# A cross-attention kernel: the queries' seven block products in transposed form, with the steady round in another order

## The chip, the cores and the metric

The kernel runs on one core of one Trainium2 chip. The metric is the device time of one launch in microseconds, as the median of several executions. The engines are TensorE (PE; its weight loads are shown as PEld), VectorE (DVE), ScalarE (ACT), GpSimd (POOL) and SyncE (SP, which here only issues DMAs). They run on their own instruction queues, each in program order, and wait for one another by semaphores.

## The reference

For each of 64 batches, with x of 256x512 and a context c of 256x384, all in float32:

```python
text_p  = x @ W_text + b_text            # queries, 256x512
audio_p = c @ W_audio + b_audio          # keys and values, 256x512
Q = layer_norm(text_p, g1, beta1)
K = layer_norm(audio_p, g2, beta2)
alpha = softmax(Q @ K.T / sqrt(512))     # 256x256
h = (alpha @ audio_p) @ W_out + b_out
out = layer_norm(h + x, g_out, beta_out)
```

## The kernel before, in words

Everything is float32 and all big products are made from fewer block products than the plain form has. The queries of a batch are a 2x2 block product (rows in two halves of 128, the inner 512 in two halves, the columns in two halves of 256) and take seven products instead of eight, each of two matmuls of 128x256. The keys (class `Thirds`) and the output projection, which is folded with the value projection (`y`, also `Thirds`), take fifteen products with columns in thirds of 171. The scores and the context's first part take seven products of 128 columns too.

The queries are class `Fork`. `SumX` makes the sums and differences of x's blocks on GpSimd (four instructions for each batch, into tile `xsum`), `weight_sums` those of the weights once (`wtsum`). Two PSUM banks, `fork[0]` and `fork[1]`, hold the four result blocks: `R`, `q1` in the first and `q2`, `q3` in the second. `Fork.seed` copies half of the bias into `R`; product one adds to `R`; `after_one` (ScalarE) copies `R` to `q1`; seven goes into `q3` and `after_seven` (ScalarE) takes it out into `s7`; six adds to `R`; `start_q3` (VectorE) writes `q3 = R + s7` and `step_r` (VectorE) moves `R` from one half of the bias to the other by `bt_step`; five adds to `R`; `after_five` (VectorE) writes `q2 = R + s7`; three, two and four finish `R`, `q1` and `q3`. `square` and `normalise` (ScalarE) then read the banks for the layer norm. `Thirds` works in the same way in four further banks (M, L, TU, N), which keys and output projection use in turn: for instance `take_m` and `start_u` (VectorE) read the two halves of bank M between `four` and `five`, and the third and fourth product of `five` write to these halves again.

The order of all work is written out by hand (a manual schedule): a prologue for the first batches, a steady round `for b in range(3, B - 3)`, 58 times, and an end. The steady round works on six batches at once: `q2`/`k2` are the queries and keys of batch b+2, `q3` is the first query product of batch b+3, `cT`/`xT`, `cs` and `x_new` are the transposed inputs and sums of batch b+3, `at` is the attention of batch b, `last` the context of b-1, `old` and `y` the output projection of b-2, `settled` the final layer norm of b-3 (`deviation`, `last_deviation`, `shift`, `settle`). A statement's place in that list sets its place in each engine's queue. The tiles of pool `work` have two buffers, those of `once` one.

The other names in the prediction: `after_six` is what follows six; `key_step`, `query_step`, `c_step`, `e_step`, `cs.add` and `x_new.add` are GpSimd sums, `z_step` are sums on VectorE or GpSimd; `turn` and `turn_e` are VectorE transposes of tiles that were stored to memory and fetched again (`store`, `fetch`, `store_e`, `fetch_e`: SP's queue); `copy_u` and `copy_n` (ScalarE) take U and N out of PSUM; `maxima` is a VectorE reduction over the scores; `affine_keys` and `affine_queries` are ScalarE. The rows of L541 are the small VectorE sums of helper `dve`, those of L1348 and L1357 are `shift` and `settle`.

Of the kernel before, what the change touches and what calls it, by code (L numbers as in the profile page):

```python
# [22 lines left out]
def kernel(  # L23
# [257 lines left out]
    def weight_sums(w_sb, n, name):  # L281

        w = [[w_sb[:, j * n : (j + 1) * n, k * H2 : (k + 1) * H2] for k in (1, 0)] for j in (0, 1)]
# [6 lines left out]
        ws = {1: w[0][0], 2: w[1][0], 3: w[1][1], 4: t[:, 3], 5: t[:, 0], 6: t[:, 1], 7: t[:, 2]}  # L290
        return {p: [ap[:, k, :] for k in range(n)] for p, ap in ws.items()}

    class SumX:

        def __init__(self, xT, engine=nc.gpsimd):
            n = DC // 2
            part = lambda i, j: xT[:, j * n : (j + 1) * n, bass.ts(i, P)]
            s = work.tile([P, 4, n, P], F32, tag="xsum", name="xsum")
            self.engine = engine
            self.steps = [  # L300
                (s[:, 2], part(0, 0), part(1, 0), ALU.subtract),
                (s[:, 0], part(1, 0), part(1, 1), ALU.add),
                (s[:, 1], s[:, 0], part(0, 0), ALU.subtract),
                (s[:, 3], part(0, 1), s[:, 1], ALU.subtract),
            ]
            ss = {
                1: part(0, 0), 2: part(0, 1), 4: part(1, 1),
                5: s[:, 0], 6: s[:, 1], 7: s[:, 2], 3: s[:, 3],
            }
            self.of = {p: [ap[:, k, :] for k in range(n)] for p, ap in ss.items()}  # L310

        def add(self, n=4):
# [404 lines left out]
    class Fork(Projection):  # L717

        R, q1 = fork[0][:, :H2], fork[0][:, H2:]
        q2, q3 = fork[1][:, :H2], fork[1][:, H2:]  # L720
# [7 lines left out]
        def seed():  # L728
            nc.scalar.copy(Fork.R, bt_sb[:, H2:])

        def product(self, n, place):
            for c, (side, w) in enumerate(zip(self.sides[n], self.weights[n])):
# [4 lines left out]
                    start=(n == 7 and c == 0),  # L737
# [7 lines left out]
        def seven(self):  # L745
            self.product(7, self.q3)
# [4 lines left out]
        def after_seven(self):  # L751
            self.s7 = once.tile([P, H2], F32, tag="s7", name="s7")
            nc.scalar.copy(self.s7, self.q3)
# [17 lines left out]
        def after_five(self):  # L771
            dve(self.q2, self.R, self.s7, ALU.add)
# [7 lines left out]
        def four(self):  # L780
            self.product(4, self.q3)

        def rest(self):
            self.three()
            self.two()
            self.four()
# [657 lines left out]
    bt_step = const.tile([P, H2], F32, tag='bt_step', name='bt_step')  # L1444
# [31 lines left out]
    xs_1.add(1)  # L1476
# [25 lines left out]
    nc.vector.tensor_tensor(bt_step, bt_sb[:, :H2], bt_sb[:, H2:], ALU.subtract)  # L1502
# [15 lines left out]
    q[1].start_q3()  # L1518
    fold_multiply(0, 3, 4)
    q[1].step_r()  # L1520
# [12 lines left out]
    xs[2].add(1)  # L1533
# [21 lines left out]
    q[1].three()  # L1555
    k2_0.start_t()
    cs[3].add(1)
    q[1].four()
# [37 lines left out]
    q2_0.start_q3()  # L1596
# [3 lines left out]
    xs[3].add(1)  # L1600
# [10 lines left out]
    q2_0.step_r()  # L1611
# [14 lines left out]
    q2_0.three()  # L1626
# [7 lines left out]
    q2_0.four()  # L1634
# [23 lines left out]
    q2_0.normalise([0])  # L1658
# [5 lines left out]
    xs[4].add(1)  # L1664
# [4 lines left out]
    q2_0.normalise([1])  # L1669
# [16 lines left out]
    q2_1.start_q3()  # L1686
    xs[4].add(1)
    k2_1.four()
    q2_1.step_r()
# [17 lines left out]
    q2_1.three()  # L1707
# [7 lines left out]
    q2_1.four()  # L1715
# [84 lines left out]
    q2_2.start_q3()  # L1800
    q2_2.step_r()
# [23 lines left out]
    q2_2.three()  # L1825
# [13 lines left out]
    q2_2.four()  # L1839
# [8 lines left out]
    xs[5].add(1)  # L1848
# [11 lines left out]
    q2_2.normalise([0])  # L1860
# [23 lines left out]
    q2_2.normalise([1])  # L1884
# [41 lines left out]
    for b in range(3, B - 3):  # L1926
        settled, old, last = att.pop(b - 3), att[b - 2], att[b - 1]
        old.context_two(0)
        old.context_two(1)
        q2 = q[b + 2]  # L1930
        old.z_part(2)
        old.copy_two()
        old.z_part(4)
        old.product_sums()
        at = att[b]
        x_old = x_rows[b - 2]
        old.z_part(3)
        old.add_c21()
        cT[b + 3] = turn_c(b + 3)
        old.copy_top()  # L1940
        q2.seven()
        old.z_step(0)
        last.context_sums()
        k2 = k[b + 2] = Thirds("k", b + 2, cs.pop(b + 2), wa_blocks, ba_sb, ba_delta)
        y = old.o
        at.affine_queries(1)
        k2.one()
        at.query_sums()
        k2.copy_n1()
        at.affine_queries(0)  # L1950
        at.query_step(0)
        old.z_step(7)
        old.z_step(1)
        old.z_step(2)
        q2.six()
        q2.after_seven()
        k2.start_t()
        at.open_scores()
        last.c_step(0)
        at.affine_queries(3)  # L1960
        k2.two()
        last.fetch_e()
        q2.start_q3()
        settled.totals()
        k2.three()
        old.z_step(3)
        k2.copy_t()
        q2.step_r()
        old.z_step(4)
        k2.start_l0()  # L1970
        at.score_part(1, 7)
        settled.deviation(1)
        k2.start_l1()
        xT[b + 3] = turn_x(b + 3)
        q2.five()
        at.affine_queries(2)
        k2.four()
        q2.after_five()
        cs[b + 3] = Sides(cT.pop(b + 3), "csum").add(0)
        x_new = SumX(xT.pop(b + 3))  # L1980
        k2.take_m()
        settled.deviation(0)
        k2.start_u()
        settled.shift(1)
        settled.last_deviation()
        cs[b + 3].add(1)
        old.z_step(5)
        var = small.tile([P, 4], F32, tag="var4", name="var")
        k2.five()
        k2.copy_n()  # L1990
        at.copy_p1()
        k[b + 1].turn([0])
        k2.leave_ends()
        q2.four()
        at.copy_p7()
        k2.copy_u()
        at.query_step(1)
        at.query_step(2)
        k2.middle_v()
        q2.square(var[:, :2], [1])  # L2000
        at.score_part(6)
        k2.leave_middle()
        q2.two()
        k2.middle_less()
        k2.leave()
        if b + 4 < B: load_c(b + 4)
        y.seed()
        at.query_step(3)
        at.add_p7(0)
        k[b + 1].turn([1])  # L2010
        if b + 4 < B: load_x(b + 4)
        k2.square(var[:, 2:], [0])
        if done: done.store()
        y.one()
        last.turn_e()
        q2.three()
        last.c_step(1)
        y.copy_n1()
        q3 = q[b + 3] = Fork(b + 3, x_new.of, wt_blocks)
        x_new.add(1)  # L2020
        cs[b + 3].add(1)
        last.open_context()
        last.weight_sums()
        at.score_part(5)
        old.z_step(6)
        k2.square(var[:, 2:], [1])
        last.e_step(0)
        q2.square(var[:, :2], [0])
        y.start_t()
        settled.settle(1)  # L2030
        at.add_p7(1)
        q[b + 1].turn()
        last.c_step(2)
        y.three()
        last.z_part(7)
        y.two()
        y.copy_t()
        att[b + 1] = Attention(b + 1)
        at.score_part(4)
        done = settled  # L2040
        scales_of(q2, k2, var)
        at.score_part(3)
        cs[b + 3].add(1)
        last.keep_z7()
        last.e_step(1)
        y.start_l1()
        last.z_part(1)
        last.e_step(2)
        q2.normalise([1])
        cs[b + 3].add(1)  # L2050
        at.score_part(2)
        att[b + 1].key_sums()
        last.c_step(3)
        y.start_l0()
        q2.normalise([0])
        last.copy_z1()
        settled.shift(0)
        x_new.add(1)
        at.maxima()
        cs[b + 3].add(1)  # L2060
        k2.normalise([0])
        y.four()
        y.take_m()
        k2.normalise([1])
        y.start_u()
        x_new.add(1)
        last.z_part(6)
        at.exponentials([0])
        at.exponentials([1])
        Fork.seed()  # L2070
        att[b + 1].affine_keys(2)
        cs[b + 3].add(1)
        att[b + 1].affine_keys(1)
        last.add_u3()
        y.five()
        cs[b + 3].add(1)
        settled.settle(0)
        att[b + 1].affine_keys(0)
        att[b + 1].affine_keys(3)
        y.plus_ends(x_old)  # L2080
        x_new.add(1)
        load_x_rows(b - 1)
        y.plus_middle(x_old, 1)
        y.last_11()
        q2.store()
        k2.seed()
        att[b + 1].key_step(0)
        k2.store()
        at.reciprocals()
        q3.one()  # L2090
        load_c_rows(b)
        y.plus_n0()
        last.z_part(5)
        q2.fetch()
        at.divide_e([1])
        at.divide_e([0])
        last.add_c22()
        y.last_01(x_old)
        at.store_e()
        q3.after_one()  # L2100
        att[b + 1].key_step(1)
        y.last_10()
        att[b + 1].key_step(2)
        k2.fetch()
        y.plus_middle(x_old, 0)
        y.last_00()
# [40 lines left out]
    q2_m3.start_q3()  # L2147
    k2_m3.four()
    at_m3.keep_p7()
    q2_m3.step_r()  # L2150
# [325 lines left out]
```

## Time and profile before

| what | value |
|---|---|
| three runs | 1336.13, 1336.77, 1336.94 us; median 1336.77 |
| profiled execution, span from first to last instruction | 1333.9 us |
| median less span | 2.87 us |
| mean granted TensorE clock | 1.000 |
| one steady round | 20.30 us |

The profiled execution is another one than the three that were timed; its own time is its span and the little that lies around it. "Busy" is the time in which an engine has an instruction in work. A row of the timeline has the start, the length, the engine, the line, the operation, what it writes and reads, and a count; a bracket says how long the engine had been idle before, and who released it. A float32 matmul appears as two records, so the two matmuls of one query product are "x4". A row of a group has total busy time and the mean length in ns behind the bar.

### The profile page before, as it was taken

What the parts mean: (1) busy time and instruction counts of PE and PEld (TensorE: products, weight loads), DVE (VectorE), ACT (ScalarE), POOL (GpSimd) and SP (SyncE); (2) the same over time, 40 slices, a digit from 0 to 9 for tenths busy, and PEclk for the clock granted to TensorE, in tenths of its full rate; (3) what the DMA queues carried; (4) which work ended last, traced back from release to release, by engine and by line L of the source; (5) the groups of instructions that cost most, each with busy time, mean ns of one, the idle gap of its engine ahead of it and who ended that gap; (6) DMA issues with size and microseconds to landing.
All of it is one profiled execution on the core that took longest, in us unless ns stands there. A gap on an engine that the chain in (4) does not pass through costs nothing.

```text
span 1333.9 us, 29733 instructions
## 1 busy us (share of the span) xinstructions
PE 1327.5 (100%) x8497; PEld 1246.6 (93%) x8497; DVE 1257.0 (94%) x3314; ACT 1174.8 (88%) x3310; POOL 1172.8 (88%) x1854
## 2 busy tenths in 40 slices
PE   9999999999999999999999999999999999999998
PEld 5899999999999999999999999999999999999996
DVE  6769999999999999999999999999999999999977
ACT  4899898898898998998988988989988989889886
POOL 5789999999998998998999999989989989999964
PEclk9999999999999999999999999999999999999999
DMA  9988898898988988988888988988889888889783
GB/s 214 250 235 239 230 268 238 241 261 237 250 251 225 261 248 241 259 248 244 249 241 239 264 236 246 260 241 246 252 225 268 246 236 258 242 241 257 213 248 116
DMA packets 448970, 322.23 MB, mean 242 GB/s; under 512 B 153765, under 2 KB 381349, under 8 KB 448806
## 3 DMA queue, kind: packets, MB, share of 16 engines
q1 hardware_dynamic: 448710, 320.20, 85.7%
q8 instruction: 68, 1.11, 0.4%
q14 instruction: 96, 0.79, 0.2%
q10 hardware_dynamic: 96, 0.13, 0.0%
HBM read 203.57 MB, written 116.65 MB: 240 GB/s over the span
## 4 chain that ended last, share of the span: by engine, by line
PE 98%; DMA 1%; DVE 0%; SPq 0%; issue 0%; POOL 0%; ACT 0%; DVEq 0%
PE ps_f L733 29%; PE ps_m L557 16%; PE ps_sc L884 14%; PE ps_n L557 11%; PE ps_u L557 8%; PE ps_z L1033 7%; PE ps_l L557 5%; PE ps_z L1095 5%; PE ps_sc L823 1%; DMA ba<-in_L_xattn_b_audio_dram 0%; DMA c<-in_ctx_dram 0%; PE ps_l L244 0%; PE ps_f L440 0%; PE ps_fold L244 0%; PE ps_m L244 0%; PE ps_sc L900 0%
## 5 line engine op out<-in xcount | busy, mean ns | idle before, releaser
L352 POOL TENSOR_TENSOR csum<-csum,cT 128x256 f32<-128x256 f32 x310 | 202.0, 652 | 0.6
L733 PE MATMUL ps_f<-wtsum,xsum 128*128 128x256 f32 x756 | 194.0, 379 | 0.0
L527 ACT ACTIVATE qT<-qT,columns 128x256 f32<-128x256 f32 x256 | 152.9, 599 | 0.0
L733 PEld LDWEIGHTS ps_f<-wtsum,xsum 128*128 128x128 f32 x756 | 131.8, 191 | 11.4 <-issue 0.7
L869 POOL TENSOR_TENSOR qsum<-qT 128x256 f32<-128x256 f32 x118 | 86.4, 732 | 58.3 <-ACT qT L527 56.7
L1158 ACT ACTIVATE junk<-yr,nm 128x512 f32<-128x512 f32 x124 | 88.6, 715 | 55.0 <-POOL nm L1140 54.8
L527 ACT ACTIVATE kT<-kT,columns 128x256 f32<-128x256 f32 x256 | 133.7, 595 | 0.4 <-DVE kT L76 0.4
L884 PE MATMUL ps_sc<-kT,qT 128*128 128x128 f32 x928 | 131.8, 275 | 0.0
L733 PE MATMUL ps_f<-wt,xT 128*128 128x256 f32 x504 | 129.5, 379 | 0.0
L1357 DVE SCALAR_TENSOR_TENSOR yr<-yr,rstd,beo 128x512 f32<-128x512 f32 x120 | 123.0, 1025 | 0.1
L884 PEld LDWEIGHTS ps_sc<-kT,qT 128*128 128x128 f32 x928 | 121.3, 192 | 0.0
L1348 DVE SCALAR_TENSOR_TENSOR yr<-yr,nm,go 128x512 f32<-128x512 f32 x124 | 109.7, 885 | 0.0
L794 ACT ACTIVATE junk<-ps_f 128x512 f32<-128x512 f32 x126 | 75.2, 597 | 35.7 <-PE ps_f L733 32.2
L884 PEld LDWEIGHTS ps_sc<-ksum,qsum 128*128 128x128 f32 x696 | 100.6, 191 | 6.0
L884 PE MATMUL ps_sc<-ksum,qsum 128*128 128x128 f32 x696 | 105.8, 275 | 0.0
L733 PEld LDWEIGHTS ps_f<-wt,xT 128*128 128x128 f32 x504 | 88.4, 190 | 6.7
L314 POOL TENSOR_TENSOR xsum<-xT 128x256 f32<-128x256 f32 x124 | 91.0, 735 | 1.9 <-DVE xT L76 1.9
L541 DVE TENSOR_TENSOR ps_l<-ps_m,t 128x171 f32<-128x171 f32 x248 | 82.8, 334 | 8.7 <-ACT t L605 3.0
L520 DVE STREAM_TRANSPOSE kT<-kq 128x512 f32<-128x512 f32 x122 | 85.4, 702 | 2.0 <-DMA kq<-kd 2.0
L488 ACT ACTIVATE kr<-kr,rstd 128x512 f32<-128x512 f32 x126 | 84.7, 727 | 0.0
L460 ACT ACTIVATE junk<-kr 128x512 f32<-128x512 f32 x126 | 80.9, 642 | 0.3
L804 ACT ACTIVATE qr<-ps_f,rstd 128x512 f32<-128x512 f32 x126 | 80.2, 690 | 0.2
(302 smaller groups left out, 4670.1 us busy)
## 6 DMA issues: line engine op xcount, KB each, us to landing
kd<-kr SPq DMA_DIRECT2D x64, 512.0 KB, 3.4
kq<-kd SPq DMA_DIRECT2D x256, 128.0 KB, 3.8
qd<-qr SPq DMA_DIRECT2D x64, 512.0 KB, 3.2
qq<-qd SPq DMA_DIRECT2D x256, 128.0 KB, 4.3
xq<-in_x_dram SPq DMA_DIRECT2D x252, 128.0 KB, 2.8
x<-in_x_dram SPq DMA_DIRECT2D x63, 512.0 KB, 5.0
out_dram<-yr SPq DMA_DIRECT2D x62, 512.0 KB, 3.8
cq<-in_ctx_dram SPq DMA_DIRECT2D x252, 96.0 KB, 2.4
```

The costliest lines, as they stand in the source:

```text
L314: self.engine.tensor_tensor(*step)
L352: nc.gpsimd.tensor_tensor(*step)
L520: nc.vector.transpose(self.T.rearrange("p k (q t j) -> p t q k j", t=self.nt, j=SQ)[:, t], self.sq[:, t * NQ : (t + 1) * NQ].rearrange("p ...
L527: nc.scalar.activation(self.T[:, k, :], self.T[:, k, :], AF.Identity, bias=bet[:, k : k + 1], scale=gam[:, k : k + 1],)
L557: nc.tensor.matmul(place, lhsT=self.sides.of[n], rhs=self.weights[n], start=(n == 14), stop=True, skip_group_check=True,)
L733: nc.tensor.matmul(place, lhsT=side, rhs=w, start=(n == 7 and c == 0), stop=True, skip_group_check=True,)
L869: nc.gpsimd.tensor_tensor(*self.steps[n])
L884: nc.tensor.matmul(self.place(t, m), lhsT=self.qsides[n][:, c], rhs=self.ksides[n][:, c], start=False, stop=True, skip_group_check=True,)
L1033: nc.tensor.matmul(self.zp[{1: 0, 2: 0, 4: 2}.get(n, 1)], lhsT=self.asides[n], rhs=self.bsides[n], start=(n == 7), stop=True, skip_group_c ...
L1158: nc.scalar.activation(junk, self.y[:, t, :], AF.Square, bias=self.nm[:, t : t + 1], accum_out=self.ssq[:, t : t + 1],)
L1348: nc.vector.scalar_tensor_tensor(row, row, self.nm[:, t : t + 1], go_sb, ALU.add, ALU.mult)
L1357: nc.vector.scalar_tensor_tensor(self.y[:, t, :], self.y[:, t, :], self.r[t], beo_sb, ALU.mult, ALU.add)
```

## The change

The block products of the queries are rearranged: the blocks of x and of the weights take each other's roles in the seven-product scheme. x's sums become three instructions, the first of them 512 columns wide; the weights' sums stay four. The roles of the PSUM blocks change: `R` and `q4` lie in `fork[1]`, `q1` and `q2` in `fork[0]`. `Fork.seed` is one copy of 512 columns: the first half of the bias goes to `R`, and the difference of the halves, which VectorE makes once in the prologue in place of `bt_step`, to `q4`. Product seven adds to that seed, so that `s7` carries the step between the halves; `step_r` is gone. `after_six` writes `q2`, `after_five` writes `q4`, and four adds to `q2`. Where the prologue and the end named the old steps they name the new ones, and three and four change places there.

```diff
-        add(t[:, 0], w[0][1], w[0][0], ALU.subtract)
-        add(t[:, 1], w[1][1], t[:, 0], ALU.subtract)
-        add(t[:, 2], w[1][1], w[0][1], ALU.subtract)
+        add(t[:, 0], w[0][1], w[1][1], ALU.add)
+        add(t[:, 1], t[:, 0], w[0][0], ALU.subtract)
+        add(t[:, 2], w[0][0], w[0][1], ALU.subtract)
         add(t[:, 3], w[1][0], t[:, 1], ALU.subtract)
...
-                (s[:, 2], part(0, 0), part(1, 0), ALU.subtract),
-                (s[:, 0], part(1, 0), part(1, 1), ALU.add),
-                (s[:, 1], s[:, 0], part(0, 0), ALU.subtract),
-                (s[:, 3], part(0, 1), s[:, 1], ALU.subtract),
+                (
+                    s[:, 0:2],
+                    xT[:, :, P:].rearrange("p (j c) l -> p j c l", j=2),
+                    xT[:, :n, :].rearrange("p c (m l) -> p m c l", m=2),
+                    ALU.subtract,
+                ),
+                (s[:, 2], part(1, 1), s[:, 0], ALU.subtract),
+                (s[:, 3], part(0, 1), s[:, 2], ALU.subtract),
...
-        R, q1 = fork[0][:, :H2], fork[0][:, H2:]
-        q2, q3 = fork[1][:, :H2], fork[1][:, H2:]
+        R, q4 = fork[1][:, :H2], fork[1][:, H2:]
+        q1, q2 = fork[0][:, :H2], fork[0][:, H2:]
...
-            nc.scalar.copy(Fork.R, bt_sb[:, H2:])
+            nc.scalar.copy(fork[1], bt_sb)
...
-                    start=(n == 7 and c == 0),
+                    start=False,
...
-        def start_q3(self):
-            dve(self.q3, self.R, self.s7, ALU.add)
-
-        def step_r(self):
-            dve(self.R, self.R, bt_step, ALU.add)
-
         def after_six(self):
-            self.start_q3()
-            self.step_r()
+            dve(self.q2, self.R, self.s7, ALU.add)
...
+    nc.vector.tensor_tensor(bt_sb[:, H2:], bt_sb[:, H2:], bt_sb[:, :H2], ALU.subtract)
...
-    nc.vector.tensor_tensor(bt_step, bt_sb[:, :H2], bt_sb[:, H2:], ALU.subtract)
```

The steady round's list is written in another order throughout. The new list, cut to the statements that the prediction speaks of:

```python
old.z_part(2); old.z_part(4); old.context_two(0); ...
q2.seven(); q2.after_seven(); k2.one(); ...
old.z_part(3); old.context_two(1); old.copy_two(); old.z_step(0); ...
q2.six(); q2.after_six(); k2.three(); ...; k2.two(); load_c(b + 4); ...
q2.five(); ...; xT[b + 3] = turn_x(b + 3); k2.four(); ...; last.fetch_e()
at.query_step(0); at.query_step(1); ...; q2.after_five(); at.score_part(1, 7); ...
k2.five(); ...; q2.three(); settled.shift(1); q2.two(); ...
k2.copy_n(); at.copy_p7(); ...; settled.last_deviation(); k2.copy_u()
k2.leave_ends(); k2.leave_middle(); k2.middle_v(); old.z_step(4); k2.middle_less()
k[b + 1].turn([1]); ...; last.turn_e(); at.score_part(6); y.one(); ...; q2.four()
cs[b + 3].add(1); ...; last.e_step(0); ...; at.add_p7(0); old.z_step(6); last.e_step(1)
y.start_t(); settled.shift(0); at.score_part(5); ...; at.add_p7(1); y.three(); last.z_part(7); ...
settled.settle(1); y.two(); at.score_part(4); load_c_rows(b); x_new.add(1); ...
y.start_l0(); ...; at.score_part(2); at.score_part(3); ...; last.z_part(1); ...
y.start_l1(); att[b + 1].q.turn(); y.four(); ...; settled.settle(0); y.take_m(); ...
y.start_u(); ...; at.maxima(); ...; last.z_part(6); ...; Fork.seed(); ...
y.five(); load_x(b + 4); ...; last.z_part(5); ...; x_new.add(1); q3.one(); ...
x_new.add(1); ...; q3.after_one(); k2.seed(); ...; att[b + 1].affine_keys(0); ...
att[b + 1].key_step(0); ...; at.store_e(); k2.fetch(); att[b + 1].key_step(2)
```

More of the change, by code (lines that the diff above doesn't have):

```diff
@@ L780, in four @@
         def four(self):
[L781 to L786, printed above, removed]
+            self.product(4, self.q2)
         def square(self, var=None, tiles=range(2)):
@@ L1633 @@
     k[1].fetch()
-    q2_0.four()
+    q2_0.three()
     at_0.score(1, 2)
@@ L1706 @@
     q2_1.two()
-    q2_1.three()
+    q2_1.four()
     at_1.affine_keys(0)
@@ L1824 @@
     q2_2.two()
-    q2_2.three()
+    q2_2.four()
     last_2.turn_e()
@@ L1948 @@
[L1948 to L1969, printed above, removed]
@@ L1988 @@
[L1988 to L2006, printed above, removed]
@@ L2026 @@
[L2026 to L2030, printed above, removed]
+        at.affine_queries(0)
+        q2.six()
+        q2.after_six()
+        k2.three()
+        last.c_step(0)
+        k2.copy_t()
+        k2.two()
+        if b + 4 < B: load_c(b + 4)
+        old.z_step(1)
+        old.z_step(3)
+        k2.start_l0()
+        old.copy_top()
+        q2.five()
+        k2.start_l1()
+        old.z_step(7)
+        at.affine_queries(1)
@@ new lines @@
+        k2.five()
+        at.query_step(2)
+        q2.three()
+        x_new = SumX(xT.pop(b + 3))
+        var = small.tile([P, 4], F32, tag="var4", name="var")
+        settled.shift(1)
+        q2.two()
+        k[b + 1].turn([0])
+        k2.copy_n()
+        at.copy_p7()
+        cs[b + 3] = Sides(cT.pop(b + 3), "csum").add(0)
+        settled.last_deviation()
+        old.z_step(5)
+        k2.copy_u()
+        k2.leave_ends()
+        k2.leave_middle()
+        k2.middle_v()
+        old.z_step(4)
@@ new lines @@
+        k2.middle_less()
+        k[b + 1].turn([1])
+        last.open_context()
+        at.query_step(3)
+        y = old.o
+        y.seed()
+        last.turn_e()
+        at.score_part(6)
+        y.one()
+        last.c_step(3)
+        q2.square(var[:, :2], [1])
+        k2.leave()
+        q2.four()
+        k2.square(var[:, 2:], [0])
+        cs[b + 3].add(1)
+        last.weight_sums()
+        y.copy_n1()
+        last.e_step(0)
+        k2.square(var[:, 2:], [1])
+        at.add_p7(0)
@@ L2055 @@
+        if done: done.store()
+        last.z_part(1)
         q2.normalise([0])
+        q2.normalise([1])
+        y.start_l1()
+        att[b + 1].q.turn()
+        y.four()
+        q3 = q[b + 3] = Fork(b + 3, x_new.of, wt_blocks)
+        settled.settle(0)
+        y.take_m()
         last.copy_z1()
-        settled.shift(0)
-        x_new.add(1)
+        y.start_u()
+        k2.normalise([0])
         at.maxima()
         cs[b + 3].add(1)
-        k2.normalise([0])
-        y.four()
-        y.take_m()
@@ L2064 @@
-        k2.normalise([1])
[L2065 to L2073, printed above, removed]
-        last.add_u3()
[L2075 to L2079, printed above, removed]
+        last.z_part(6)
+        cs[b + 3].add(1)
+        last.e_step(2)
@@ L2080 @@
+        Fork.seed()
+        load_x_rows(b - 1)
+        k2.normalise([1])
+        att[b + 1].affine_keys(3)
+        y.five()
+        if b + 4 < B: load_x(b + 4)
+        last.add_u3()
+        last.z_part(5)
+        q2.store()
+        x_old = x_rows[b - 2]
         y.plus_ends(x_old)
         x_new.add(1)
-        load_x_rows(b - 1)
+        q3.one()
+        at.exponentials([0])
+        last.add_c22()
         y.plus_middle(x_old, 1)
+        k2.store()
+        cs[b + 3].add(1)
+        y.plus_n0()
@@ L2084 @@
+        x_new.add(1)
+        at.exponentials([1])
+        cs[b + 3].add(1)
         y.last_11()
-        q2.store()
+        att[b + 1].affine_keys(2)
+        q3.after_one()
         k2.seed()
-        att[b + 1].key_step(0)
[L2088 to L2094, printed above, removed]
+        y.last_10()
+        q2.fetch()
+        att[b + 1].affine_keys(0)
+        at.reciprocals()
+        at.divide_e([0])
```

189 lines of the change are left out of this document (81 added, 108 removed).

## The prediction

> **What bounds the kernel now.** I read the page first (busy time, chain of waits), then busy time by stretches, then one steady round engine by engine on the timeline.
>
> ```profile
> span 1333.9 us, 29733 instructions
> PE 1327.5 (100%) x8497; PEld 1246.6 (93%) x8497; DVE 1257.0 (94%) x3314; ACT 1174.8 (88%) x3310; POOL 1172.8 (88%) x1854
> PE 98%; DMA 1%; DVE 0%; SPq 0%; issue 0%; POOL 0%; ACT 0%; DVEq 0%
> 95.00:1272.00 1177.00, 1177.00 (x7770) 1125.81 (x7769) 1149.07 (x3073) 1060.21 (x3016) 1070.54 (x1682) 1.00 0.87 246
> ```
>
> In the last row, by stretches, the columns are window, length, busy time of PE, weight load, DVE, ACT and POOL, then granted clock, DMA share and GB/s. The reader is to see that TensorE has no idle time in the 1177 us of the 58 steady rounds (1177/58 = 20.29 each), at full granted clock, and that 98% of the chain is PE. Divided by 58 the others are busy for 19.41 (weight load), 19.81 (DVE), 18.28 (ACT) and 18.46 (POOL): DVE is 0.48 us per round short of full, ACT 2.0, POOL 1.8.
>
> A busy PE need not be a PE at its peak, since its ends are modelled, so I look at starts:
>
> ```profile
> 640.52 1.03 PE L733 MATMUL ps_f<-wt,xT 128*128 128x256 f32 x4
> 641.38 0.38 PE L1033 MATMUL ps_z<-esum,asum 128*128 128x128 f32 x2
> 641.60 1.03 PE L1095 MATMUL ps_z<-eT,c 128*128 128x256 f32 x4
> ...
> 651.84 0.61 PE L884 MATMUL ps_sc<-ksum,qsum 128*128 128x128 f32 x4
> 652.28 1.03 PE L733 MATMUL ps_f<-wt,xT 128*128 128x256 f32 x4
> 653.14 0.74 PE L557 MATMUL ps_n<-wao,zsum 128*128 128x171 f32 x4
> 653.73 1.03 PE L733 MATMUL ps_f<-wt,xsum 128*128 128x256 f32 x4
> ...
> 660.82 1.03 PE L733 MATMUL ps_f<-wt,xT 128*128 128x256 f32 x4
> ```
>
> First column start, second length. From start to start a block product of the queries takes 0.86, a z product 0.22, a score product 0.44 to 0.445, two thirds products 0.58 to 0.59 (0.29 each). A round holds 7 query products (6.06), 30 thirds products (8.72), 7 score products (3.11), 7 z products (1.56) and two context products of 0.43 (0.87): 20.32, and the round is 20.30 (640.52 to 660.82). So the rows leave no hidden wait.
>
> **The change part by part.** *TensorE.* The transposed form has the same seven products of two 128x256 matmuls with the same operand shapes; three, two and four only swap places. Difference: 0. A gain therefore cannot come from the steady rounds; the other engines' savings count only as cover.
>
> *Engine work per round.*
>
> ```profile
> L541 DVE TENSOR_TENSOR ps_f<-ps_f,bt_step 128x256 f32<-128x256 f32 x63 | 26.7, 424 | 0.0
> L314 POOL TENSOR_TENSOR xsum<-xT x124: 721/727/1181, 36.7 to 1266.9; 128x256 f32<-128x256 f32 x124
> L866 POOL TENSOR_TENSOR ksum<-kT x59: 1268/1278/1287, 93.6 to 1271.5; 128x512 f32<-128x512 f32 x59
> 659.88 0.38 ACT L729 COPY ps_f<-bt 128x256 f32<-128x256 f32 x1
> 36.82 0.58 ACT L253 COPY wao<-ps_l 128x512 f32<-128x512 f32 x1
> ```
>
> DVE loses step_r (0.42). POOL's four x sums of 0.73 (2.92) become one of the shape of key step 0 (1.28) and two of 0.73: 2.74, so 0.18 less. ACT's seed grows from 256 to 512 columns; no row seeds 512 columns, the nearest is a 512-column copy of 0.58, so +0.20 (bounds 0 and +0.3). With nothing else, DVE 19.4, ACT 18.5 and POOL 18.3 of 20.30: none becomes the bound by its sum. The four weight sums keep number and width.
>
> *Seven now adds to a seeded bank* (start flag gone), so it waits for the seed. In the steady round the seed already precedes product one of the same batch, and seven comes a z pair and a context product later: hidden, 0. With step_r gone the path from six to five is one DVE step instead of two; in the new order only three (0.29) and two (0.58) stand between them, 0.87.
>
> ```profile
> 652.48 0.30 DVE L541 TENSOR_TENSOR ps_sc<-ps_sc,sc 128x128 f32<-128x128 f32 x1 [0.16 <-PE ps_sc L884]
> ```
>
> This row of DVE waited for the score product above: it reads the result 0.20 us after the next product started (652.48 against 652.28). Add the step itself, 0.42 as in the row of step_r, the same shape: 0.62 of 0.87, so five is on time by about 0.25 if DVE is free at that moment, and in my layout it waits there for six.
>
> *Prologue, once.*
>
> ```profile
> 28.92 1.28 DVE L449 TENSOR_TENSOR kr<-ps_f,ba 128x512 f32<-128x512 f32 x2
> 30.23 0.38 ACT L729 COPY ps_f<-bt 128x256 f32<-128x256 f32 x1 [2.84 <-DVE kr L449]
> 30.45 1.03 PE L733 MATMUL ps_f<-wtsum,xsum 128*128 128x256 f32 x4
> ```
>
> The seed used to wait for the second of two evictions (the bank of tile 0); now it needs only the first (28.92 + 0.64 = 29.56), and with 0.6 it is done at 30.2, before the first seven at 30.45. The bias subtraction ahead of it takes the place of one x sum on DVE. Bounds once for the whole run: -0.3 to +0.4 us; I take 0. The later stretches (prologue rounds and end) issue the same products, with less on DVE.
>
> *The steady round's other order* is the part that can cost, because each round repeats it 58 times: 0.05 us of stall per round is 2.9 us. I laid the new order out with PE as the clock and searched each product for what it needs. Cover found, smallest first: the second score product waits for query step 0 on POOL (about 0.25); five for after_six (0.25); y.three for z step 6 and start_t (0.3); z 7 for e step 0 (0.4). The queues: SP issues load_c ahead of fetch_e now; of two DMA rows
>
> ```profile
> ed<-e SPq DMA_DIRECT2D x61, 256.0 KB, 3.9
> eq<-ed SPq DMA_DIRECT2D x244, 64.0 KB, 2.2
> ```
>
> e is stored some 2.3 us after q3.one, landed at 6.6, fetched by 8.4 and there by 10.6; turn_e comes at 11.7, so 1 us of cover. The loads of c rows, x rows, x and the output store follow behind; nothing of this round reads them. POOL ends the round waiting some 1.5 us for affine_keys(0), which ACT now issues after q3.after_one, so that lateness of the sums ahead of it is taken up there.
>
> The place that decides is the DVE run from the eviction of k's last product to y.start_u, which must read bank M before the third product of y.five overwrites it:
>
> ```profile
> 649.77 0.30 ACT L422 ACTIVATE log<-ssq,eps 128x2 f32<-128x2 f32 x1
> ...
> L1084 DVE TENSOR_TENSOR zsum<-zsum,ps_z 128x128 f32<-128x128 f32 x174 | 47.0, 270 | 0.0
> L1348 DVE SCALAR_TENSOR_TENSOR yr<-yr,nm,go x124: 732/746/1164, 101.8 to 1323.0; 128x512 f32<-128x512 f32 x124
> 654.53 0.88 DVE L1357 SCALAR_TENSOR_TENSOR yr<-yr,rstd,beo 128x512 f32<-128x512 f32 x1
> ...
> 657.29 1.05 DVE L1348 SCALAR_TENSOR_TENSOR yr<-yr,nm,go 128x512 f32<-128x512 f32 x1
> 658.26 0.68 DVE L938 TENSOR_REDUCE nmx<-ps_sc 128x2 f32<-128x512 f32 x1
> 658.86 0.32 DVE L541 TENSOR_TENSOR m<-ps_m,bao_delta 128x171 f32<-128x171 f32 x1
> 659.21 0.34 DVE L541 TENSOR_TENSOR ps_u<-ps_m,m 128x171 f32<-128x171 f32 x1
> 659.77 1.22 DVE L1357 SCALAR_TENSOR_TENSOR yr<-yr,rstd,beo 128x512 f32<-128x512 f32 x1
> 659.95 0.74 PE L557 MATMUL ps_m<-wao_thirds,zT 128*128 128x171 f32 x4
> ```
>
> Before, start_u ends at 659.55 and the product starts at 659.95: 0.40 to spare, over a PE distance that the new order keeps (8.97 from the end of k.five: products three, two and four 2.60, five score products 2.23, y.one to y.four 2.90, three z products 0.67, two products of y.five 0.58). In the new order maxima leaves this run (658.26 to 658.86: 0.60), the wait of 0.16 goes, z step 4 joins (0.27 long) and so does settle(0), one of the row operations L1348 and L1357, 0.73 to 1.22 long in these rows. The next instruction starts 0.08 before the end of one (657.29 + 1.05 against 658.26), so I count 0.2 and 0.65 to 1.14. On ACT, copy_u now stands behind last_deviation, two small instructions (the first 0.30 long), part of them before the product is done: 0 to 0.5 late, I take 0.2. The spare becomes 0.40 + 0.60 + 0.16 - 0.2 - 0.2 - (0.65 to 1.14) = +0.11 to -0.38 with the other row operations as long as before (shift(0) 0.97, settle(1) 0.80 of DVE's time), and up to 0.47 better where these two come down to 0.65. What sets their length is read here:
>
> ```profile
> 659.72 0.73 POOL L314 TENSOR_TENSOR xsum<-xsum,xT 128x256 f32<-128x256 f32 x1
> 660.40 0.91 POOL L352 TENSOR_TENSOR csum<-csum,cT 128x128 f32<-128x128 f32 x1
> ```
>
> settle(0) was issued at 659.77, just after a POOL sum had begun; it ended 0.59 after the next POOL sum's start (660.40 + 0.59 = 660.99) and held that one up (0.91). A row operation of DVE waits for the POOL instruction in progress. The Trainium skill's page "SBUF — State Buffer", section "Who interferes with whom", says the same: a VectorE instruction with two SBUF inputs and a GpSimd one that reads SBUF exclude each other, and the second fully blocks. By that rule the new 512-wide x sum, which stands between e_step(1) and settle(1), could block settle for its whole length.
>
> Laying the new order along these rows, shift(0) is issued 0.25 before e_step(1) begins, settle(1) about 0.15 before the wide x sum begins, settle(0) about 0.1 before a csum begins: each gets in first. Then shift(0) takes 0.76, settle(1) 0.67 and settle(0) 0.62 to 0.65 of DVE's time, 0.34 less for the first two than before, and 0.11 + 0.34, about 0.45 us of spare is left. I take 0 for the order. Sum: 0 (PE) + 0 (prologue) + 58 x 0 = the time before. The profiled execution's span is 1333.9; the three runs shown have a median of 1336.77, 2.87 more, which I carry over unchanged: 1336.8.
>
> **The rivals.** *A, slower: the DVE run ends after y.five needs bank M.* One mechanism: shift(0), settle(1) or settle(0) loses its race with a POOL sum. For it: the margins of those races are 0.1 to 0.15 us by my layout, whose errors are as large; the wide x sum doubles one possible wait (1.28). Against: each is won on paper, and before, DVE was fuller (19.81) without a stall. It decides once start_u ends over 0.05 us late. From the bound of -0.38: a typical stall of 0.2 gives 58 x 0.2 = 11.6, 1348 us; the bound itself 22, 1359 us. If settle(1) meets the full wide sum it is 0.7 or more, about 1378 us; I think that unlikely.
>
> *B, faster: PE has room that its busy time hides.* The page "Perfetto Trace Analysis" of the Trainium skill, section "Identifying the Most-Contended Engine", holds that matmul busy time misleads and weight-load busy time is the better measure; by it 0.88 us per round (20.29 - 19.41) might be free, 51 us in all, 1286 us. The trace speaks against it: the pitches above add up to the whole round. Only waits at the prologue or the end are left, 6.4 us of PE idle time in the span (1333.9 - 1327.5), of which the change touches next to nothing. A gain that can be measured would be some 3 to 4 us, 1333 us.
>
> *C, the work saved does nothing:* that is the forecast itself, as all of it lies beside PE.
>
> **How the numbers follow.** Within 0.2% (2.7 us, about what a measurement here can tell from no change): 0.62, my forecast, with a range of its own of 1335.6 to 1338.2. A: 0.34, of which about a third over 0.22 us per round. B: 0.04. The range leaves out that third of A and most of B: low 1335.0, high 1336.8 + 58 x 0.22 = 1349.5.
>
> **What would show it.** Right: 20.30 us per steady round with PE busy throughout; DVE near 19.4, or lower by shorter row operations, with waits on PE; POOL's xsum lines with 128x512 at 1.28; ACT's seed near 0.58; PE's instruction count unchanged. Wrong by A: PE idle before y's products into ps_m, released by DVE ps_u (start_u), in every round, and settle or shift rows of 1.0 us or more. Wrong elsewhere: PE waiting on POOL qsum ahead of the scores, or on DVE ps_f (after_six) ahead of five.

## Result: 43 us slower, and the profile after

The changed kernel takes 1379.41 us (median of four runs, 1378.90 to 1380.71), the kernel before 1336.63 beside it (1336.13 to 1336.94): a ratio of 1.032, 95% interval 1.0306 to 1.0335. The forecast of 1336.8 and its range to 1349.5 are both missed, on the slow side.

From the page of the changed kernel, the span, the busy times and the chain:

```profile
span 1377.1 us, 29662 instructions
PE 1361.8 (99%) x8497; PEld 1250.3 (91%) x8497; DVE 1258.1 (91%) x3250; ACT 1186.6 (86%) x3310; POOL 1150.9 (84%) x1792
PE 71%; DVE 10%; DMA 9%; ACT 5%; issue 2%; SPq 1%; POOL 1%; DVEq 0%
```

The same 8497 matmul records now need 43.2 us more. PE is still "busy" for 99%, but only 71% of the chain is PE; before, it was 98%. The busy share hides most of the loss: 34.3 of the 43.2 us are counted as busy (1361.8 against 1327.5). In the rows below, four records of a thirds product last 0.74 at a usual pitch of 0.58, so the next can start up to 0.16 late before PE shows any idle time. The view of waits names the two places in the steady rounds (columns: total us, times, longest):

```profile
PEld ps_z L1025 <- DVE zT L545: 18.2, 57, 0.3
PEld ps_m L561 <- DVE ps_u L545: 15.2, 56, 0.5
```

Both are waits of the weight load, each once in nearly every one of the 58 rounds. The starts on PE's timeline show what each costs:

```profile
660.43 0.74 PE L561 MATMUL ps_n<-wao_thirds,zsum 128*128 128x171 f32 x4
661.18 0.85 PE L561 MATMUL ps_m<-wao_thirds,zT 128*128 128x171 f32 x4
661.87 0.45 PE L561 MATMUL ps_u<-wao_thirds,zT 128*128 128x171 f32 x2
...
664.99 0.74 PE L561 MATMUL ps_n<-wa,csum 128*128 128x171 f32 x4
665.78 0.49 PE L1025 MATMUL ps_z<-eT,c 128*128 128x128 f32 x2
666.11 0.60 PE L1087 MATMUL ps_z<-eT,c 128*128 128x256 f32 x2
```

The first place is y.five: its third product starts 0.75 behind the start of the pair ahead of it, not 0.58, and the next 0.69 behind that, not 0.58. The second is z_part(3), right behind k.one: 0.79 instead of 0.58, and the next 0.33 instead of 0.22. So a late weight load costs its wait and 0.10 to 0.11 more at the matmul behind it (called the restart below). I summed every start-to-start distance less the median distance of its shape. A steady round has 0.28 at y.five (in 54 rounds), 0.32 at z_part(3) and 0.04 at k.four (each in 57), and is 20.94 long instead of 20.30. That makes 36 us in the steady rounds. In the first 110 us the sum is 8.1 against 3.4 before, and at the end 2.6 against nothing before: single waits, 1.7 of the end's at one product. Most of the rest at the end is one more wait at y.five.

Why y.five waits: DVE, then POOL.

```profile
656.58 0.74 DVE L1349 SCALAR_TENSOR_TENSOR yr<-yr,rstd,beo 128x512 f32<-128x512 f32 x1
658.10 1.23 DVE L76 STREAM_TRANSPOSE qT<-qq 128x1024 f32<-128x1024 f32 x1
659.26 1.25 DVE L1349 SCALAR_TENSOR_TENSOR yr<-yr,rstd,beo 128x512 f32<-128x512 f32 x1
660.43 0.32 DVE L545 TENSOR_TENSOR m<-ps_m,bao_delta 128x171 f32<-128x171 f32 x1
660.78 0.34 DVE L545 TENSOR_TENSOR ps_u<-ps_m,m 128x171 f32<-128x171 f32 x1
...
656.74 1.72 POOL L318 TENSOR_TENSOR xsum<-xT 128x512 f32<-128x512 f32 x1
658.42 1.54 POOL L356 TENSOR_TENSOR csum<-csum,cT 128x256 f32<-128x256 f32 x2
659.22 1.60 POOL L356 TENSOR_TENSOR csum<-csum,cT 128x256 f32<-128x256 f32 x2
```

settle(1), at 656.58, won its race with the wide x sum and took 0.74. settle(0), at 659.26, came 0.04 after a csum had begun at 659.22 (the last two rows overlap: this csum is the second of the one and the first of the other). It ended at 660.51, 0.55 behind that sum's end (658.42 + 1.54 = 659.96), and start_u is done only at 661.12. Over 55 rounds the medians are 0.03 after the csum's start and 1.25 for the row.

Why z_part(3) waits: the last row of this DVE stretch is add_c21.

```profile
665.01 0.51 DVE L711 SCALAR_TENSOR_TENSOR yr<-ps_l,x 128x342 f32<-128x342 f32 x1
665.45 0.28 DVE L545 TENSOR_TENSOR zT<-ps_z,u 128x128 f32<-128x128 f32 x1
665.65 0.97 DVE L76 STREAM_TRANSPOSE cT<-cq 128x768 f32<-128x768 f32 x1
```

add_c21 reads the block zp[2] of ps_z1 and ends at 665.73; z_part(3), at 665.78, writes the block zp[1] of the same PSUM tile. The two touch different columns, and the product waits all the same. In the order before, z_part(3) stood ahead of add_c21.

### The profile page after: what moved, and what is told of

Read it like the earlier page. It is cut to its first block, busy times and chain, and to the rows that moved or that the text cites. A ratio compares the mean times of both kernels' runs of the same rounds, so it can differ in the third digit from the quotient of the medians.

```text
span 1377.1 us, 29662 instructions
## 1 busy us (share of the span) xinstructions
PE 1361.8 (99%) x8497; PEld 1250.3 (91%) x8497; DVE 1258.1 (91%) x3250; ACT 1186.6 (86%) x3310; POOL 1150.9 (84%) x1792
## 4 chain that ended last, share of the span: by engine, by line
PE 71%; DVE 10%; DMA 9%; ACT 5%; issue 2%; SPq 1%; POOL 1%; DVEq 0%
PE ps_f L737 19%; PE ps_m L561 14%; PE ps_sc L876 11%; PE ps_n L561 7%; PE ps_u L561 6%; DMA qd<-qr 5%; PE ps_l L561 4%; DMA qq<-qd 4%; PE ps_z L1025 4%; DVE yr L711 4%; PE ps_z L1087 3%; ACT qr L796 2%; DVE zT L545 2%; DVE n L545 1%; DVE u L545 1%
## 5 line engine op out<-in xcount | busy, mean ns | idle before, releaser
L356 POOL TENSOR_TENSOR csum<-csum,cT 128x256 f32<-128x256 f32 x310 | 193.3, 632 | 9.8
L531 ACT ACTIVATE kT<-kT,columns 128x256 f32<-128x256 f32 x256 | 151.1, 594 | 0.4 <-DVE kT L76 0.4
L531 ACT ACTIVATE qT<-qT,columns 128x256 f32<-128x256 f32 x256 | 140.5, 596 | 0.0
L858 POOL TENSOR_TENSOR ksum<-kT 128x512 f32<-128x512 f32 x59 | 75.4, 1277 | 56.6 <-ACT kT L531 56.6
L876 PE MATMUL ps_sc<-kT,qT 128*128 128x128 f32 x928 | 122.3, 275 | 0.0
L1340 DVE SCALAR_TENSOR_TENSOR yr<-yr,nm,go 128x512 f32<-128x512 f32 x124 | 118.8, 959 | 0.0
L318 POOL TENSOR_TENSOR xsum<-xT 128x512 f32<-128x512 f32 x62 | 105.4, 1699 | 1.9 <-DVE xT L76 1.9
L1015 POOL TENSOR_TENSOR esum<-eT 128x256 f32<-128x256 f32 x59 | 43.2, 733 | 69.3 <-DVE eT L76 68.1
L1076 POOL TENSOR_TENSOR zsum<-zsum,zT 128x128 f32<-128x128 f32 x116 | 79.3, 684 | 19.7 <-DVE zsum L1076 19.7
L318 POOL TENSOR_TENSOR xsum<-xT,xsum 128x256 f32<-128x256 f32 x124 | 90.4, 729 | 0.2
```

The lines of the kernel that those rows point to most:

```text
L318: self.engine.tensor_tensor(*step)
L356: nc.gpsimd.tensor_tensor(*step)
L531: nc.scalar.activation(self.T[:, k, :], self.T[:, k, :], AF.Identity, bias=bet[:, k : k + 1], scale=gam[:, k : k + 1],)
L876: nc.tensor.matmul(self.place(t, m), lhsT=self.qsides[n][:, c], rhs=self.ksides[n][:, c], start=False, stop=True, skip_group_check=True,)
L1340: nc.vector.scalar_tensor_tensor(row, row, self.nm[:, t : t + 1], go_sb, ALU.add, ALU.mult)
```

## Experiments

Times are medians. Each ratio is against the kernel before in the same session (1336.73, 1336.38 and 1335.94 us in the three), with its 95% interval. Theory 1 is the race of settle(0), theory 2 the wait of z_part(3) on add_c21. The main rival is the form itself (wide sum, wide seed, other products).

**1. settle(0) moved behind add_u3.**

```diff
-        settled.settle(0)
         y.take_m()
 ...
         last.add_u3()
+        settled.settle(0)
```

> The changed kernel (1379.4 us) with one statement moved: settle(0) of the steady round stands behind add_u3 instead of ahead of take_m. Theory 1 (y.five waits for start_u, which is late behind settle(0) at 1.25 us): the 0.28 us lost a round at y.five goes, 58 rounds x 0.28 = 16 us, less what the later settle(0) costs plus_ends and add_c21 (up to 0.1 to 0.2 us a round): 1363 to 1374. Rival (the wide form of x's sums or the wider seed costs the time, the order nothing): 1379 within 1. Rival (DVE is simply full): the stall goes from y.five to the next one, 1379 or above.

1396.03 us, 1.0444 (1.0428 to 1.0459): slower by another 16.6. The wait at y.five is gone from the trace, so it was settle(0)'s. Two others have grown in its place:

```profile
PEld ps_z L1025 <- DVE zT L545: 58.0, 114, 0.5
647.50 1.30 DVE L1349 SCALAR_TENSOR_TENSOR yr<-yr,rstd,beo 128x512 f32<-128x512 f32 x1
649.14 0.27 DVE L545 TENSOR_TENSOR zT<-ps_z,z 128x128 f32<-128x128 f32 x1
```

settle(0) lost its race here too (1.30) and pushed back everything behind it. Now z_part(2) waits for add_c22 as well, 114 waits in all instead of 57. By its number the rival that calls DVE full held, but this run cannot tell a full DVE from one more lost race; experiment 6, which moves the same row the other way, can.

**2. add_c21 moved behind z_part(3).**

```diff
         old.context_two(0)
-        old.add_c21()
 ...
         old.z_part(3)
+        old.add_c21()
```

> The changed kernel with one statement moved: add_c21 stands behind z_part(3) instead of ahead of it. Theory 2 (z_part(3) writes one column block of the bank ps_z1 and waits for add_c21 to have read another block of the same bank): the 0.32 us lost a round between k.one and context_two goes, 58 x 0.32 = 18.5 us: 1361, up to 1368 if copy_two and z_step(0) then come later. Rival (DVE lateness itself, which the next wait on DVE takes over): 1377 to 1380.

1361.29 us, 1.0186 (1.0169 to 1.0203): 18.1 less, as theory 2 asked. The row PEld ps_z is gone from the waits; this one is left:

```profile
PEld ps_m L561 <- DVE ps_u L545: 12.6, 48, 0.5
657.03 0.74 PE L561 MATMUL ps_n<-wa,csum 128*128 128x171 f32 x4
657.61 0.38 PE L1025 MATMUL ps_z<-eT,c 128*128 128x128 f32 x2
657.83 0.60 PE L1087 MATMUL ps_z<-eT,c 128*128 128x256 f32 x2
```

z_part(3) starts 0.58 behind k.one's last pair and the next 0.22 behind it: both at their usual pitch.

**3. Both moves.**

> Both moves together. Theories 1 and 2 add: 1379.4 - 16 - 18.5 = 1345, up to 1355 if the moved settle(0) delays plus_ends. Left are the first 110 us (4.7) and the last (1.7): 1343 is the least. Rival (form, not order): 1379.

1377.69 us, 1.0307 (1.0291 to 1.0322). The sum that both theories asked for (1345 to 1355) is missed: the moves do not add, since the first is a bad one. z_part(2) loses 0.26 and 0.10 a round, and the product five, k.four and their restarts some 0.25 more.

**4. The new form with the old order of the round.**

```diff
         last.fetch_e()
-        q2.start_q3()
+        q2.after_six()
 ...
         k2.copy_t()
-        q2.step_r()
```

(and three and four exchanged, one x_new.add less; all else of the changed kernel kept)

> The new form of the seven products, the one seed copy and the three sums of x, everywhere as in the changed kernel, but the steady round's statements in the order of before (after_six in the place of start_q3, step_r gone, three and four exchanged, one x_new.add less). Order theory: the steady round is free of stalls as before, 1336.8 plus what the first 110 us and the end lost (4.7 and 1.7): 1337 to 1344. Rival (the form itself: the wide sum of 1.70 us against DVE, or the seed of 0.59 us): 0.3 us a round or more stay, 1355 to 1379.

1382.98 us, 1.0346 (1.0331 to 1.0361). The order theory as I had put it fails: the new form in the old order is no faster. But it is a different wait, one per round:

```profile
PEld ps_f L737 <- ACT ps_f L753: 38.3, 60, 1.5
645.22 1.13 PE L737 MATMUL ps_f<-wtsum,xsum 128*128 128x256 f32 x4 [0.45 <-ACT ps_f L753]
643.99 0.91 ACT L952 ACTIVATE e<-e,rden 128x256 f32<-128x256 f32 x2
644.80 0.37 ACT L753 COPY ps_f<-ps_f 128x256 f32<-128x256 f32 x1
```

Seven waits for after_one (L753), which stands behind divide_e (L952) on ACT and ends at 645.17. It costs 0.61, and 0.10 at the restart, in each round. Seven writes q4 and after_one reads R; in the new form these two share one PSUM tile, in the old one q3 and R did not. That is theory 3.

**5. The old form with the new order of the round.**

> The kernel before (1336.7 us) with its own form of the seven products, its seed and its four sums of x, and in the steady round the changed kernel's order of statements (three and four exchanged, the fourth sum of x beside the third place). Theory (the new order brings both waits, whatever the form): z_part(3) still waits for add_c21, 0.32 us a round, and y.five for start_u up to 0.28: 1355 to 1374, likelier the upper half, since step_r (0.42) makes DVE later still. Rival (the order is harmless to the old form, which has a bank less to wait for): 1337 to 1340.

1379.46 us, 1.0318 (1.0303 to 1.0334): the time of the changed kernel, without any of its new form.

```profile
PEld ps_z L1033 <- DVE zT L541: 18.1, 57, 0.3
PEld ps_f L733 <- DVE ps_f L541: 15.1, 59, 0.6
```

z_part(3) loses the same 18.1 us in 57 waits. So that wait belongs to the order alone. The second one is another: the product five waits for step_r, which only the old form has (first row below), and loses 0.15 and 0.10 a round, with 0.10 more at k.four. y.five, which the theory had waiting here too, waits in two rounds only:

```profile
645.55 0.42 DVE L541 TENSOR_TENSOR ps_f<-ps_f,bt_step 128x256 f32<-128x256 f32 x1
658.13 0.71 DVE L1357 SCALAR_TENSOR_TENSOR yr<-yr,rstd,beo 128x512 f32<-128x512 f32 x1
658.23 1.19 POOL L352 TENSOR_TENSOR csum<-csum,cT 128x256 f32<-128x256 f32 x1
```

settle(0) stands at the same place of the order and wins its race: it is issued 0.11 ahead of this csum and takes 0.71 (medians of 55 rounds). settle(0) comes 2.68 behind settle(1) in both kernels, but that csum begins 2.78 behind settle(1) here and 2.64 in the changed kernel, where the one wide x sum stands in the place of two narrow ones. So the lost race at y.five took the new form as well as the new order, by these rows through the sums of x. That the two kernels' times agree is luck.

**6. Experiment 2 with settle(0) ahead of the turn of q.**

```diff
         y.start_l1()
+        settled.settle(0)
         att[b + 1].q.turn()
 ...
-        settled.settle(0)
         y.take_m()
```

> The second experiment's kernel (add_c21 behind z_part(3), 1361.3 us) with settle(0) ahead of the turn of q instead of behind it. Theory 1: it is issued 0.3 us ahead of a boundary between two GpSimd sums and ends 0.59 behind that, so start_u ends about 0.26 us earlier; y.five loses nothing, 58 x 0.27 = 16 us less: 1345 to 1348. Rival (DVE is full, any order of its rows moves the wait to the next place, as moving settle(0) behind add_u3 did): 1358 to 1365. Rival (the race is lost here too, behind the wide sum of 1.72 us): 1365 or above.

1353.01 us, 1.0117 (1.0100 to 1.0134): 8.3 less than experiment 2, half of what theory 1 asked. So DVE is not simply full.

```profile
PEld ps_m L561 <- DVE ps_u L545: 2.4, 13, 0.4
PEld ps_sc L876 <- DVE ps_sc L545: 5.4, 10, 1.3
644.95 1.14 DVE L1349 SCALAR_TENSOR_TENSOR yr<-yr,rstd,beo 128x512 f32<-128x512 f32 x1
641.41 0.71 DVE L76 STREAM_TRANSPOSE eT<-eq 128x512 f32<-128x512 f32 x1 [0.64 <-DMA eq<-ed]
```

The wait at y.five falls from 48 rounds to 13, as theory 1 has it; with the restarts it had cost 12.8 us in experiment 2, and 2.6 are left. settle(0) takes 0.91 here (median of 56 rounds; 1.14 in the round shown). What ate part of the gain is in the last row: in this round turn_e waits for e to come back from memory, and the score product behind it waits for DVE. Such waits of score products come in ten places, and DVE's waits for e in ten (5.5 us; one of 1.1 in the kernel before). So the 1 us that the forecast counted as cover for e does not hold in every round of this order.

**7. Experiment 4 with after_one ahead of divide_e on ACT.**

```diff
         q3.one()
+        q3.after_one()
 ...
         at.store_e()
-        q3.after_one()
```

> The fourth experiment's kernel (new form, old order, 1383.0 us) with one statement moved: after_one of the next pair stands directly behind q3.one, ahead of divide_e on ScalarE, instead of behind it. Theory 3 (in the new form seven writes q4, which shares a bank with R, and so waits for after_one, which reads R; 0.61 us and 0.10 at the restart in each round, and 1.27 at the end): 1383.0 - 58 x 0.71 - 1.4 = 1340.4, up to 1344. Rival (ScalarE or DVE are late altogether in the old order with the new form): 1370 or above.

1341.74 us, 1.0038 (1.0024 to 1.0052): 41.2 us less by one statement.

```profile
110.00:1270.00 1160.00, 1160.00 (x7662) 1112.81 (x7662) 1114.63 (x2970) 1057.72 (x2977) 1047.62 (x1601) 1.00 0.86 246
646.67 0.33 ACT L753 COPY ps_f<-ps_f 128x256 f32<-128x256 f32 x1
646.93 0.92 ACT L952 ACTIVATE e<-e,rden 128x256 f32<-128x256 f32 x2
647.29 1.03 PE L737 MATMUL ps_f<-wtsum,xsum 128*128 128x256 f32 x4
```

In the first row, by stretches, PE is busy in all 1160 us with 7662 records, against 7660 in the kernel before and 7433 in the changed kernel in the same stretch. after_one is done at 647.00 and seven starts on its pitch at 647.29. The new form costs nothing in the steady rounds here. What is left against the kernel before (5.4 us; 6.0 between the two profiled spans) lies at the two ends: 4.1 more lost in the first 110 us, 2.2 at the end.

**8. Experiment 7 with after_seven of the first pair behind the loop moved up.**

```diff
     k2_m3.one()
+    q2_m3.after_seven()
 ...
-    q2_m3.after_seven()
     q2_m3.six()
```

> The seventh experiment's kernel with after_seven of the first pair behind the loop moved up behind k2.one. Theory 3 again: six writes R, in q4's bank, and waits for after_seven, which reads q4; that cost 1.59 and 0.10 us once, at the end: 1.7 us below the seventh experiment, 1338.7. Rival (six waits for something else there, by dependence or by ScalarE's own lateness): no change against the seventh.

1341.32 us, 1.0035 (1.0022 to 1.0048), against 1341.74. In the profile six no longer waits (it starts 0.32 behind its predecessor at 1281.07; in the changed kernel 1.90 behind, after 1.43 us of idle PE released by after_seven). The timed runs overlap (1340.48 to 1342.14 against 1341.24 to 1342.42), so a gain of 1.7 us is not shown by them. In the profiled execution the first 110 us lost 9.2 instead of 7.5, in single waits ahead of the first query product that come and go between executions, which hides it there.

**9. Experiment 4 with R and q1 in one PSUM bank, q4 and q2 in the other.**

```diff
-    fork = [p_all.tile([P, H], F32, tag=f"f{n}", name=f"ps_f{n}") for n in range(2)]
+    pair = p_all.tile([P, 2, H], F32, tag="f", name="ps_f")
+    fork = [pair[:, n, :] for n in range(2)]
 ...
-        R, q4 = fork[1][:, :H2], fork[1][:, H2:]
-        q1, q2 = fork[0][:, :H2], fork[0][:, H2:]
+        R, q4 = fork[0][:, :H2], fork[1][:, :H2]
+        q1, q2 = fork[0][:, H2:], fork[1][:, H2:]
```

(seed, square and normalise name the halves to suit)

> The fourth experiment's kernel (new form, old order, after_one in its old place, 1383.0 us), with only the places in PSUM changed: R and q1 in one bank, q4 and q2 in the other, so that a tile of rows is read as two halves from two banks. Bank theory: seven no longer shares a bank with R; its 0.71 us a round goes, and so do the waits of seven and six in the first 110 us (4.1) and at the end (2.2 to 2.9). But two now writes q1 in R's bank, which the square of tile 1 reads at that time (0.37 us, and 0.10 at the restart, by the seventh experiment's rows): 1383.0 - 41.4 - 6.5 + 27 = 1362. Rival (waits follow the columns, not the bank): two does not wait, and seven did not either: 1383. Rival (seven waited only because ScalarE is late): seven's wait stays, 1383 to 1400.

1414.16 us, 1.0584 (1.0565 to 1.0603): none of the theories. Both waits are there:

```profile
639.07 1.13 PE L740 MATMUL ps_f<-wtsum,xsum 128*128 128x256 f32 x4 [0.28 <-ACT ps_f L756]
648.82 1.13 PE L740 MATMUL ps_f<-wt,xT 128*128 128x256 f32 x4 [0.33 <-ACT junk L789]
638.64 0.38 ACT L756 COPY ps_f<-ps_f 128x256 f32<-128x256 f32 x1
648.08 0.60 ACT L789 ACTIVATE junk<-ps_f 128x512 f32<-128x512 f32 x1 [0.56 <-PE ps_f L740]
```

There are two waits for the square (0.50 and 0.10 a round), as the bank theory said. But seven waits for after_one still (0.45 and 0.10), though after_one now reads and writes one bank and seven writes the other. What they share is the tile: for this experiment the two banks were allocated as one. With two tiles, as in the kernel before, seven had no such wait. The waits follow the allocated PSUM tile, neither its columns nor its bank. The tile is a unit of the program; whether the chip itself would need these waits, no run here shows. The Trainium skill's page "PSUM — Partial Sum Buffer", section "PSUM bank collisions raise a hardware error", asks for a semaphore by bank and quadrant, not by address. That would explain the waits of z_part(3) and seven in the changed kernel, where tile and bank are the same; it doesn't ask for the one here.

**10. Experiment 9 with the square of tile 1 behind two.**

> The ninth experiment's kernel with the square of tile 1 behind the product two instead of ahead of it. Bank theory: two has nothing to wait for; none of the three waits is left, and the form costs nothing where its banks are apart: 1341.7 (the seventh experiment) - 4.1 at the start - 2.2 at the end = 1335.4, up to 1342 if ScalarE, now some 1.1 us later at this point, passes its lateness on. Rival (the 512-wide sum, the wider seed or the two-bank reads cost time of their own): 1345 or above.

1452.23 us, 1.0872 (1.0855 to 1.0889). The bank theory fails again. Per round seven loses 0.65, four 0.36 (it waits for the square now) and a product of y into ps_u 0.49 (it waits for DVE), each with 0.10 at the restart: 1.81 x 58 = 105 us.

## Why the prediction was wrong

Three steps failed, each of which took a wait at 0.

**The order at 0, first wait: settle(0).** The forecast's margin was "about 0.1 before a csum begins"; it came 0.04 after one (0.03 in the median). The mechanism is rival A as written: the row took 1.25 instead of 0.65, about the 0.45 of spare was used up and start_u was late. Its price was 0.28 a round in 54 rounds, 15 us in all, near the typical 11.6 given for A. Experiments 1 and 6 show that the wait belongs to settle(0). The prediction had feared that the wide x sum would block settle(1); that race was won (0.74). But the sums of x set when the csum behind them begins, and experiment 5 shows that with the old sums the same order wins the race by 0.11. A layout good to some 0.1 us could not decide it, as the prediction itself says of its margins.

**The order at 0, second wait: z_part(3).** The search "each product for what it needs" looked at data and at the bank of y.five, and did not see that z_part(3) shares a PSUM tile with what add_c21 reads. No rival contains it, and it alone leads out of the stated range (1336.8 + 18 = 1355, an estimate). It was 0.32 a round, 18 us, the larger part; experiment 2 takes it away alone, and experiment 5 brings it to the old form.

**Seven at 0, and the prologue at 0 (bounds -0.3 to +0.4).** In the changed kernel's steady rounds seven is indeed free. In the prologue it isn't:

```profile
48.42 0.36 ACT L753 COPY ps_f<-ps_f 128x256 f32<-128x256 f32 x1 [2.28 <-PE ps_f L737]
48.92 0.89 PE L737 MATMUL ps_f<-wtsum,xsum 128*128 128x256 f32 x3 [0.59 <-ACT ps_f L753]
30.62 0.59 ACT L733 COPY ps_f<-bt 128x512 f32<-128x512 f32 x1 [3.46 <-DVE kr L453]
28.23 1.75 DVE L318 TENSOR_TENSOR xsum<-xT 128x512 f32<-128x512 f32 x1
```

The first two rows are the wait on after_one. The forecast asked only for the seed, and not which other readers seven's new place would have. The last two are the first seed, forecast at 30.2 and done at 31.21, since DVE's 512-wide x sum took 1.75 while POOL made the weight sums, and the bias subtraction ahead of it 0.88. This is read from the rows alone; no experiment changes the prologue. Together with the end it is 6 to 7 us. Experiment 4 gives the same step's price where the order does not allow for it: 0.71 a round, 41 us. So the new form, unmended, does not go with the old order, and the new order (after_one early, seven late) avoids that wait and brings the other two.

**Right:** no gain from PE, whose 8497 records are unchanged; the seed at 0.59 (forecast 0.58). Busy time in one steady round of the changed kernel, by stretches:

```profile
641.44:662.38 20.94, 20.88 (x137) 19.50 (x135) 19.87 (x53) 18.47 (x53) 18.09 (x29) 1.00 0.87 240
```

ACT's 18.47 and POOL's 18.09 are near the forecast 18.5 and 18.3. DVE's 19.87, not 19.4, holds settle(0)'s wait. Rival B (hidden room on PE) got no support: where no wait was left, in experiment 7, the round kept its 20.30 us.

The experiments point to no version that beats the kernel before. The best, 7 and 8, are 0.35 to 0.38% behind it.

## What to carry to other kernels

Where an order is rearranged around a saturated TensorE, list for each product all readers and writers of the PSUM tile that it writes, not only of its columns, and keep them ahead in the order by at least the lateness of their engine. A margin of 0.1 us on paper in a race between two engines is no margin: price it at its loss. When an early waiter is mended, look first at what the moved instruction stands ahead of now; moving settle(0) back cost nearly as much as moving add_c21 gained (16.6 against 18.1 us).

## What the runs showed of the hardware

- A matmul whose weight load waited costs its wait and about 0.10 us more at the next one: medians of 0.101 to 0.104 at z_part(3), y.five and seven. A wait of 0.2 is thus one of 0.3. At k.four, where no start ahead of it is late, 0.04 to 0.06 are lost in the changed kernel and experiments 1, 2 and 6; what loses them is open.
- A DVE row operation with two SBUF inputs that is issued 0.04 us after a POOL sum began ends 0.55 behind that sum's end (659.96 and 660.51); in experiment 6, issued into the wide sum, it ended at 646.09, again 0.55 behind that sum's end (643.82 + 1.72 = 645.54). The Trainium skill's page "SBUF — State Buffer", section "Who interferes with whom", calls this an exclusive lock, and the trace agrees.
- The wide x sum on POOL was counted as 1.28, and took 1.70 on average:

```profile
L318 POOL TENSOR_TENSOR xsum<-xT 128x512 f32<-128x512 f32 x62 | 105.4, 1699 | 1.9 <-DVE xT L76 1.9
L318 POOL TENSOR_TENSOR xsum<-xT 128x512 f32<-128x512 f32 x62 | 79.6, 1283 | 1.9 <-DVE xT L76 1.9
```

The second row is of experiment 7, where no row operation of DVE stands beside it in the steady rounds: 1.28, as counted. In the changed kernel settle(1) holds it up, some 0.4 us each time.
